# Moving the degrees and layernorm statistics of the incoming sample from behind the first to behind the fifth product of a step

## Chip, cores, metric

One core of one Trainium2 chip. The metric is the device time of one execution in microseconds (us). Each figure is a median of several executions. All compared executions are of the fast state (none is more than 1.5% above the fastest of its kernel); the one single execution, whose state is unknown, is named where it is used. A granted clock is the mean share of TensorE's full clock in an execution. Ratios are the mean time of one kernel's fast runs over that of the other's of the same rounds, so they are not quite the ratio of the medians quoted.

## The reference, cut to what matters

```python
h = jnp.maximum(_layernorm(x, axis=-1), 0.0)          # x: (64, 256, 768)
adj = adj.astype(h.dtype); radj = jnp.swapaxes(adj, 1, 2)   # (64, 256, 256) of 0 and 1
deg, rdeg = adj.sum(-1), radj.sum(-1)                 # 1 where 0, when divided by
ctx = adj  @ (h @ Wadj.T + badj) / deg  \
    + radj @ (h @ Wrev.T + brev) / rdeg \
    + h @ Wself.T + bself
out = x + ctx + rel        # rel: terms of rank 1 in deg and rdeg for this data
```

## The kernel before

For each of the 64 samples the three 768x768 weight products are done as 15 smaller products of combined blocks, a fast matrix multiplication. Each of the 15 is six fp32 matmuls of 128x256, which the profile shows as 12 records (x12). Products bear the numbers of the algorithm: product 5 stands at place 0 of a step, product 10 at place 4, product 14 at place 11. In the profile a product has the name of the bank that it is summed in (y, v, x, u, z, w, t). The y that waits below is product 13, at place 13. A loop over samples is software-pipelined. Step `t` does the products of sample `M = t`, aggregates sample `A = t+1` over its adjacency (`pa`), and loads and normalises sample `N = t+2`. Everything between two products is issued by `others_of_step`. In the traces an engine works in the order of the program: in step 30 VectorE reads v only at 1514.84, behind the waiting statistics, though TensorE finished v near 1508.1, and GpSimd does b2-a only behind the power, for which it was idle 10.26 us.

```python
def statistics(b):                       # VectorE, one instruction on GpSimd
    ...
    for c in range(C):
        for n in range(2):
            nc.vector.bn_stats(stats[:, c, n, :], s["x"][:, c, ts(n, HO)])
        nc.vector.bn_aggr(v[:, c, MEAN : RSTD + 1], stats[:, c, :, :])
    nc.vector.tensor_scalar(v[:, :, RSTD], ...)                     # L269
    nc.gpsimd.tensor_tensor(v[:, :, RSTD], ..., half, op=ALU.pow)   # L270
    ...                                                # junk: is adj only 0 and 1?
    nc.vector.tensor_scalar(t[:, :, 0:2], t[:, :, 3:5], ...)        # L276, needs degrees
    ...                                                # L277, reciprocal, copy L280

def normalise(b):
    for c in range(C):
        nc.vector.tensor_scalar(hx[:, c, :], s["x"][:, c, :], ...)            # L309
        nc.scalar.activation(s["hi"][:, c, :], hx[:, c, :], AF.Copy, scale=rstd)
        nc.vector.scalar_tensor_tensor(s["lo"][:, c, :], hx[:, c, :], ...)    # L313

def others_of_step(A, N, k):             # behind the product at place k of 15
    if N is not None and k == 0:
        degrees(N)                       # ScalarE: int32 to fp32r with row sums
        statistics(N)
    if A is not None:
        if 1 <= k <= F:                  # F is 6
            aggregate(A, k - 1)          # four matmuls into pa, a multiply into X
        if k == 3:
            self_features(A)             # GpSimd: xT, then relu on ScalarE
            ...
    if N is not None:
        if k == 8:
            spread(N)                    # TensorE transposes the columns (pt)
        if k == 9:
            normalise(N)

def step(t):
    load(N)                              # x has 3 buffers: waits for the store of sample t-1
    for k, (n, bank, row, reads, needs) in enumerate(ORDER):
        for name in needs:
            combine_left(M, name)        # GpSimd sums of left blocks
        ...
        product(M, n, banks[bank], start, row)
        for read in reads:
            add_out(M, banks[bank], *read)   # VectorE: x += or -= the product
        others_of_step(...)
```

Of the kernel before, what the change touches and what calls it, by code (L numbers as in the profile page):

```python
# [81 lines left out]
def kernel(  # L82
# [54 lines left out]
    def main_path(main: ExitStack):  # L137
# [108 lines left out]
        def load_xt(b):  # L246
            s = S[b]
            s["xT"] = pool1.tile([P, F, L], F32, tag="xT", name=f"xT_{b}")
            nc.sync.dma_start(s["xT"], xt_v[b])

        def degrees(b):

            s = S[b]
            s["a"] = pool2.tile([P, C, 2, L], F32R, tag="a", name=f"a_{b}")
            for c in range(C):
                for k in range(2):
                    nc.scalar.activation(  # L257
                        s["a"][:, c, k, :], s["adj"][:, c, k, :], AF.Copy, accum_out=tok[b % 2][:, c, 4 - k : 5 - k]
                    )

        def statistics(b):
            s = S[b]
            t, v = tok[b % 2], cols[b % 2]
            stats = pool2.tile([P, C, 2, 6], F32, tag="stats", name=f"stats_{b}")
# [4 lines that stand above are left out]
            nc.vector.tensor_scalar(v[:, :, RSTD], v[:, :, RSTD], EPS, None, op0=ALU.add)  # L269
            nc.gpsimd.tensor_tensor(v[:, :, RSTD], v[:, :, RSTD], half, op=ALU.pow)  # L270
            junk = pool1.tile([P, C, L], BF16, tag="junk", name=f"junk_{b}")
            a = s["adj"][:, :, 1, :]
            nc.vector.scalar_tensor_tensor(
                junk, a, 1.0, a, op0=ALU.is_equal, op1=ALU.not_equal, accum_out=others[:, b : b + 1]
            )
            nc.vector.tensor_scalar(t[:, :, 0:2], t[:, :, 3:5], 0.0, None, op0=ALU.is_gt)  # L276
            nc.vector.tensor_scalar(v[:, :, RDEG : RRDEG + 1], t[:, :, 3:5], 1.0, None, op0=ALU.max)  # L277
            nc.vector.reciprocal(v[:, :, RDEG : RRDEG + 1], v[:, :, RDEG : RRDEG + 1])
            to = v.rearrange("p c (k r) -> p c k r", k=2)[:, :, :, :NROW]
            nc.vector.tensor_copy(to, t.unsqueeze(2).to_broadcast([P, C, 2, NROW]))  # L280

        def spread(b):

            s = S[b]
            v = cols[b % 2]
            pt = ps1.tile([P, P], F32, tag="pt", name=f"pt_{b}")
            nc.tensor.transpose(pt, v.rearrange("p c k -> p (c k)"), ident)  # L287
            s["tokT"] = pool3.tile([P, P], F32R, tag="tokT", name=f"tokT_{b}")
            nc.scalar.activation(s["tokT"], pt, AF.Copy)
            line = pool2.tile([P, P], F32, tag="line", name=f"line_{b}")  # L290
            nc.scalar.activation(line, pt, AF.Copy)
            d = dram.tile([4, C, P], F32, tag="d", name=f"d_{b}")
            for c in range(C):
                nc.sync.dma_start(d[:, c, :], line[c * 64 + MEAN : c * 64 + RRDEG + 1, :])
            s["row"] = pool1.tile([P, 4, L], F32, tag="row", name=f"row_{b}")
            nc.sync.dma_start(
                s["row"].rearrange("p k i -> p (k i)"), d.rearrange("k c p -> (k c p)").partition_broadcast(P)
            )

        def normalise(b):  # L300

            s = S[b]
            v = cols[b % 2]
            s["hi"] = pool1.tile([P, C, H], F32R, tag="hl0", name=f"hi_{b}")
            s["lo"] = pool1.tile([P, C, H], F32R, tag="hl1", name=f"lo_{b}")
            hx = pool1.tile([P, C, H], F32, tag="hx", name=f"hx_{b}")
            for c in range(C):
                rstd = v[:, c, RSTD : RSTD + 1]
                nc.vector.tensor_scalar(  # L309
                    hx[:, c, :], s["x"][:, c, :], v[:, c, MEAN : MEAN + 1], 0.0, op0=ALU.subtract, op1=ALU.max  # L310
                )
                nc.scalar.activation(s["hi"][:, c, :], hx[:, c, :], AF.Copy, scale=rstd)  # L312
                nc.vector.scalar_tensor_tensor(  # L313
                    s["lo"][:, c, :], hx[:, c, :], rstd, s["hi"][:, c, :].bitcast(F32), op0=ALU.mult, op1=ALU.subtract
                )

        def new_left(b):
            S[b]["X"] = pool2.tile([P, F, 3, L], F32, tag="X", name=f"X_{b}")

        def self_features(b):  # L320

            s = S[b]
            xT, row = s["xT"], s["row"]
            parts = ((nc.gpsimd, 0, F),) if b > 0 else ((nc.gpsimd, 0, F // 2), (nc.vector, F // 2, F))
            for eng, f0, f1 in parts:
                for k, op in ((0, ALU.subtract), (1, ALU.mult)):
                    v = xT[:, f0:f1, :]
                    eng.tensor_tensor(v, v, row[:, k : k + 1, :].to_broadcast([P, f1 - f0, L]), op=op)  # L328
            nc.scalar.activation(s["X"][:, :, 2, :], xT, AF.Relu)

        def aggregate(b, f):
            s = S[b]
            pa = ps2.tile([P, 512], F32, tag="pa", name=f"pa_{b}_{f}")
            k = 0
            for c in range(C):
                for part in ("hi", "lo"):
                    nc.tensor.matmul(  # L337
                        pa, s[part][:, c, ts(f, P)], s["a"][:, c, :, :].rearrange("p s i -> p (s i)"),
                        start=(k == 0), stop=(k == 2 * C - 1),
                    )  # L340
                    k += 1
            nc.vector.tensor_mul(  # L342
                s["X"][:, f, 0:2, :].rearrange("p s i -> p (s i)"), pa, s["row"][:, 2:4, :].rearrange("p s i -> p (s i)")
            )
# [87 lines left out]

        def others_of_step(A, N, k):

            if N is not None and k == 0:
                degrees(N)
                statistics(N)
            if A is not None:
                if k == 1:
                    new_left(A)  # L440
                if 1 <= k <= F:
                    aggregate(A, k - 1)
                if k == 3:
                    self_features(A)
                    if N is not None:
                        load_xt(N)
            if N is not None:
                if k == 8:
                    spread(N)
                if k == 9:  # L450
                    normalise(N)

        def step(t):
# [7 lines left out]
            for k, (n, bank, row, reads, needs) in enumerate(ORDER):  # L461
                for name in needs:
                    combine_left(M, name)
                if t == 0:
                    first_step(k)
                start = bank not in banks
                if start:
                    pool, tag = (ps1, bank) if bank in ("x", "y") else (ps3, "q")
                    banks[bank] = pool.tile([P, 512], F32, tag=tag, name=f"{bank}_{M}")[:, :NB]
                product(M, n, banks[bank], start, row)  # L470
                for read in reads:
                    add_out(M, banks[bank], *read)
                for at in range(k, k + 1 if k + 1 < len(ORDER) else k + 4):
                    others_of_step(A if has_a else None, N if has_n else None, at - wait)
                if t == B - 1 and k == 2:
                    flag_others()
                if k == 13:
                    nc.sync.dma_start(out_v[M][:, 0, :], S[M]["x"][:, 0, :])
# [175 lines left out]
```

## Time and profile before

| | before |
|---|---|
| time, median of the first 4 runs | 3161.97 us (3150.85 to 3170.08) |
| span of the profiled execution | 3137.0 us |
| TensorE busy, VectorE busy | 94%, 43% |
| start-up up to step 2, then a steady step | 158 us, 47.76 us (median) |
| stop of pa in a steady step, mean | 0.47 us |
| stop of y in a steady step | 2.17 us |

A "stop" below is measured on TensorE's timeline. It is the distance from the start of one group of matmuls to the start of the next, less what that distance is where nothing waits. Where nothing waits, it repeats to 0.03 us. The prediction shows the lines of the profile that carry this, but for one of VectorE's (line waited for, total us, times, longest):

```profile
DVE stats L267 <- DMA x<-in_x_dram: 270.9, 61, 6.1
```

### The profile page before, as it was taken

How to read it: one execution, taken by the hardware profiler on the slowest of the kernel's cores; microseconds unless marked ns; L12 is line 12 of the kernel's file. 1: busy time of each engine (PE TensorE's matmuls, PEld its weight loads, DVE VectorE, ACT ScalarE, POOL GpSimd, SP SyncE). 2: the span in 40 equal slices, each digit the busy share in tenths (PEclk: the TensorE clock that was granted, in tenths of full speed). 3: DMA queues.
4: the chain of work that ended last, by engine and by line, in shares of the span. 5: the costliest groups of instructions: out<-in, count | busy, mean ns of one | idle time of the engine just before them, and what ended most of it. 6: DMA issues, size and time to landing. Idle time of an engine off the chain costs nothing.

```text
span 3137.0 us, 33335 instructions
## 1 busy us (share of the span) xinstructions
PE 2951.0 (94%) x13514; PEld 2535.8 (81%) x13514; DVE 1344.4 (43%) x2526; ACT 362.9 (12%) x845; POOL 1891.5 (60%) x903
## 2 busy tenths in 40 slices
PE   6899999999999999999999999999999999999999
PEld 4788888888888888888888887888788888888888
DVE  7543444444444434444444444444444444444441
ACT  2110111111111101111111110111111110111100
POOL 3755666566566656665665565656655666666563
PEclk8999999999999999999999999999999999999999
DMA  7122111221221221122212212222122122121210
GB/s 246 61 81 73 65 71 68 74 78 61 81 78 61 79 79 62 71 72 77 71 66 76 78 61 71 71 75 73 61 81 78 61 72 77 70 71 66 76 61 21
DMA packets 126053, 233.25 MB, mean 74 GB/s; under 512 B 7092, under 2 KB 68276, under 8 KB 125896
## 3 DMA queue, kind: packets, MB, share of 16 engines
q1 hardware_dynamic: 125896, 231.08, 21.2%
q8 instruction: 108, 1.77, 0.2%
q14 instruction: 49, 0.40, 0.0%
HBM read 180.46 MB, written 50.59 MB: 74 GB/s over the span
## 4 chain that ended last, share of the span: by engine, by line
PE 66%; DVE 21%; DMA 7%; ACT 4%; issue 1%; POOL 1%; SPq 0%; DVEq 0%; ACTq 0%; POOLq 0%
PE y L363 14%; PE x L363 14%; PE w L363 11%; PE z L363 10%; PE pa L337 10%; DVE hx L309 8%; DVE lo L313 5%; DMA x<-in_x_dram 4%; ACT hi L312 4%; PE u L363 3%; PE v L363 3%; DMA out_dram<-x 2%; DVE x L376 2%; DVE x L378 2%; DVE stats L267 2%
## 5 line engine op out<-in xcount | busy, mean ns | idle before, releaser
L363 PE MATMUL y<-w,X 128*128 128x256 f32 x2304 | 545.1, 387 | 124.0 <-DVE x L378 119.6
L363 PEld LDWEIGHTS y<-w,X 128*128 128x128 f32 x2304 | 434.4, 193 | 200.1 <-DVE x L378 137.8
L358 POOL TENSOR_TENSOR X<-X 128x768 f32<-128x768 f32 x190 | 345.8, 1820 | 293.8 <-PE pt L287 275.5
L270 POOL TENSOR_TENSOR cols<-cols,half 128x2 f32<-128x2 f32 x64 | 68.5, 1070 | 633.4 <-DVE cols L269 622.8
L328 POOL TENSOR_TENSOR xT<-xT,row 128x1536 f32<-128x1536 f32 (+1 forms) x128 | 440.0, 3437 | 12.1 <-DMA row<-d 7.1
L337 PE MATMUL pa<-a,hi 128*128 128x512 f32 x768 | 358.8, 467 | 23.2 <-DVE X L342 19.1
L363 PE MATMUL x<-w,X 128*128 128x256 f32 x1536 | 352.8, 379 | 1.6 <-POOL X L358 1.6
L363 PE MATMUL x<-w,a2+b 128*128 128x256 f32 x1536 | 352.6, 379 | 0.0
L358 POOL TENSOR_TENSOR a2+b<-X,a2+b 128x768 f32<-128x768 f32 x128 | 234.6, 1833 | 149.7 <-PE z L363 92.7
L363 PEld LDWEIGHTS x<-w,X 128*128 128x128 f32 x1536 | 287.3, 190 | 42.5 <-POOL X L358 2.0
L363 PEld LDWEIGHTS x<-w,a2+b 128*128 128x128 f32 x1536 | 282.6, 190 | 39.6
L342 DVE TENSOR_TENSOR X<-pa,row 128x512 f32<-128x512 f32 x384 | 263.8, 687 | 101.0 <-PE pa L337 101.0
L337 PE MATMUL pa<-a,lo 128*128 128x512 f32 x768 | 303.9, 396 | 0.5 <-DVE lo L313 0.5
L309 DVE TENSOR_SCALAR hx<-x,cols 128x768 f32<-128x768 f32 x128 | 261.0, 2039 | 0.0
L267 DVE BATCH_NORM_STATS2 stats<-x 128x6 f32<-128x384 f32 x256 | 127.1, 538 | 270.9 <-DMA x<-in_x_dram 270.9
L257 ACT ACTIVATE a<-adj 128x256 fp32r<-128x256 int32 x256 | 103.5, 406 | 1011.8 <-DMA adj<-in_adj_dram 1011.8
L358 POOL TENSOR_TENSOR a2+b<-X 128x768 f32<-128x768 f32 x64 | 162.4, 2538 | 96.3 <-PE x L368 96.3
L313 DVE SCALAR_TENSOR_TENSOR lo<-hx,cols,hi 128x768 fp32r<-128x768 f32 x128 | 152.1, 1188 | 137.4 <-ACT hi L312 137.4
L337 PEld LDWEIGHTS pa<-a,hi 128*128 128x128 f32 x768 | 145.8, 190 | 70.9 <-DVE X L342 40.6
L363 PE MATMUL w<-w,X 128*128 128x256 f32 x768 | 178.5, 382 | 7.8 <-DVE x L376 7.8
L363 PE MATMUL y<-w,b0+b 128*128 128x256 f32 x768 | 178.2, 382 | 7.2 <-DVE x L378 4.4
L363 PE MATMUL z<-w,a2+b 128*128 128x256 f32 x768 | 177.9, 382 | 2.9 <-DVE x L376 2.9
(87 smaller groups left out, 4078.7 us busy)
## 6 DMA issues: line engine op xcount, KB each, us to landing
x<-in_x_dram SPq DMA_DIRECT2D x64, 768.0 KB, 4.4
xT<-in_x_t_dram SPq DMA_DIRECT2D x64, 768.0 KB
out_dram<-x SPq DMA_DIRECT2D x128, 384.0 KB, 2.3
adj<-in_adj_dram SPq DMA_DIRECT2D x64, 512.0 KB, 3.5
row<-d SPq DMA_DIRECT2D x64, 512.0 KB, 4.3
w<-in_Wadj_dram SPq DMA_DIRECT2D x6, 768.0 KB
w<-in_Wself_dram SPq DMA_DIRECT2D x5, 768.0 KB
w<-in_Wrev_dram SPq DMA_DIRECT2D x4, 768.0 KB, 9.7
```

What stands on the lines that cost most here:

```text
L257: nc.scalar.activation(s["a"][:, c, k, :], s["adj"][:, c, k, :], AF.Copy, accum_out=tok[b % 2][:, c, 4 - k : 5 - k])
L267: nc.vector.bn_stats(stats[:, c, n, :], s["x"][:, c, ts(n, HO)])
L270: nc.gpsimd.tensor_tensor(v[:, :, RSTD], v[:, :, RSTD], half, op=ALU.pow)
L309: nc.vector.tensor_scalar(hx[:, c, :], s["x"][:, c, :], v[:, c, MEAN : MEAN + 1], 0.0, op0=ALU.subtract, op1=ALU.max)
L312: nc.scalar.activation(s["hi"][:, c, :], hx[:, c, :], AF.Copy, scale=rstd)
L313: nc.vector.scalar_tensor_tensor(s["lo"][:, c, :], hx[:, c, :], rstd, s["hi"][:, c, :].bitcast(F32), op0=ALU.mult, op1=ALU.subtract)
L328: eng.tensor_tensor(v, v, row[:, k : k + 1, :].to_broadcast([P, f1 - f0, L]), op=op)
L337: nc.tensor.matmul(pa, s[part][:, c, ts(f, P)], s["a"][:, c, :, :].rearrange("p s i -> p (s i)"), start=(k == 0), stop=(k == 2 * C - 1),)
L342: nc.vector.tensor_mul(s["X"][:, f, 0:2, :].rearrange("p s i -> p (s i)"), pa, s["row"][:, 2:4, :].rearrange("p s i -> p (s i)"))
L358: (eng or nc.gpsimd).tensor_tensor(L[name], L[x], L[y], op=op)
L363: nc.tensor.matmul(ps, l[:, f, :], W[n][:, f, :], start=(start and f == 0), stop=(row is None and f == F - 1), skip_group_check=not start,)
L376: nc.vector.tensor_add(o, o, ps)
```

## The change

The intent is to take the statistics, which wait for a late load of x, away from the beginning of the step, where VectorE must soon read products and multiply pa.

```diff
         def others_of_step(A, N, k):
 
-            if N is not None and k == 0:
-                degrees(N)
-                statistics(N)
             if A is not None:
 ...
             if N is not None:
+                if k == 4:
+                    degrees(N)
+                    statistics(N)
                 if k == 8:
                     spread(N)
```

## The prediction

> **What bounds the kernel now.** I read the page first, then the table of waits by engine, then one steady step in the timeline of each engine.
>
> ```profile
> span 3137.0 us, 33335 instructions
> PE 2951.0 (94%) x13514; PEld 2535.8 (81%) x13514; DVE 1344.4 (43%) x2526; ACT 362.9 (12%) x845; POOL 1891.5 (60%) x903
> ```
>
> TensorE is busy for 94% of the span, and its products head the chain that ended last. So this change can only win back time in which TensorE stood still. The table of waits says for whom it stood still (line waited for, total us, times, longest):
>
> ```profile
> PE y L363 <- DVE x L378: 124.0, 61, 4.4
> PE pa L337 <- DVE X L342: 19.1, 25, 3.5
> PEld y L363 <- DVE x L378: 137.8, 60, 2.3
> PEld pa L337 <- DVE X L342: 40.6, 61, 4.2
> ```
>
> There are two regular stops, one of each kind in a step of one sample. The large one (y, the fourteenth product) is 2.0 us in nearly every step. The small one (pa, the adjacency product) shows 25 times on the matmul row but 61 times on the weight-load row: most of these stops are too short to open a gap between modelled matmuls. Step 30 in the timeline, TensorE first:
>
> ```profile
> 1497.57 2.86 PE L363 MATMUL y<-w,X 128*128 128x256 f32 x12 [2.00 <-DVE x L378]
> ...
> 1503.08 2.75 PE L363 MATMUL y<-w,b0+b 128*128 128x256 f32 x12
> ...
> 1512.70 2.75 PE L363 MATMUL u<-w,X 128*128 128x256 f32 x12
> 1516.17 0.50 PE L337 MATMUL pa<-a,hi 128*128 128x512 f32 x1 [0.72 <-DVE X L342]
> ```
>
> The step begins at 1503.08 with product 5. The third group of pa (1516.17) must wait for a buffer: pa has two, and the first is free only when VectorE has multiplied it into X. VectorE in the same stretch:
>
> ```profile
> 1505.87 0.42 DVE L376 TENSOR_TENSOR x<-x,y 128x256 f32<-128x256 f32 x1 [2.17 <-PE y L363]
> 1511.31 1.02 DVE L267 BATCH_NORM_STATS2 stats<-x 128x6 f32<-128x384 f32 x2 [5.01 <-DMA x<-in_x_dram]
> ...
> 1514.78 0.15 DVE L280 COPY cols<-tok 128x20 f32<-128x20 f32 x1
> 1514.84 0.68 DVE L376 TENSOR_TENSOR x<-x,v 128x512 f32<-128x512 f32 x1
> 1515.43 0.68 DVE L342 TENSOR_TENSOR X<-pa,row 128x512 f32<-128x512 f32 x1
> 1516.04 0.41 DVE L376 TENSOR_TENSOR x<-x,x 128x256 f32<-128x256 f32 x1
> ```
>
> The statistics block stands right behind the first product, where its x has not landed: VectorE idles 5.01 us, then works 3.53 us (1511.31 to 1514.84). Only then may it read v, which TensorE finished near 1508.1. The multiply of pa(0) ends at 1516.1, and TensorE resumes at 1516.17. The x load is late because its buffer is that of the sample just stored:
>
> ```profile
> 1503.73 0.34 SPq L483 DMA_DIRECT2D out_dram<-x  x1
> 1507.07 0.39 SPq L242 DMA_DIRECT2D x<-in_x_dram  x1
> ```
>
> That is 3.34 us for the store to finish and 4.2 us for the load to land.
>
> [...] the read of v sits behind the waiting statistics some 6.7 us after v was done (1508.1 to 1514.84). [...] the 384 KB store takes from 2.3 us (in the common step) to over 3.3 us to release the load. [...] after the 2.0 us stop the y product normally takes 2.86 us, but 4.1 to 4.5 us in five of sixty steps. [...] In the trace, hx (L309) takes 0.61 us alone and about 2.0 us beside a GpSimd sum.
>
> **The change part by part.** Nothing is added or removed. Four ScalarE conversions and eleven VectorE instructions (3.53 us) and one GpSimd power (1.07 us) move, per step, from behind product 5 to behind product 10. The order of the built programs confirms the place: on VectorE after the multiply of pa(3), before the read of w; on GpSimd after the two xT operations; on ScalarE after the relu.
>
> (a) *The stop of pa, steps 2 to 61.* I took start-to-start differences on TensorE for each place in the step. Apart from the two stops and the cold products they agree to 0.03 us. From u over pa(2) to its next matmul they should be 2.82 us (2.40 + 0.42, as at the neighbouring groups). Summed over the 60 steps, the excess is 28.2 us, 0.47 us per step, from 0.0 to 2.16. It tracks the start of the statistics: the best step starts them 7.20 us into the step with no stop, step 30 at 8.23 with about 1.0. All of that should go: after the change VectorE multiplies pa(0) as soon as it is made, near 9 us less queueing, while TensorE needs the buffer only at 12.
>
> (b) *What the block costs in its new place.* Multiply of pa(3): 1520.93 to 1521.6. Block of 3.53 us with no wait, for x landed 10 us earlier: to 1525.2. Read of w delayed from 1523.5 to 1525.2, multiply of pa(4) to 1526.2. TensorE needs the read of w only at 1527.88 (w again), pa(3)'s buffer at 1526.95, and the next z is read at 1527.15. The closest margin is about 1 us, so nothing on the path: cost 0.
>
> (c) *GpSimd.* Before, the power kept it idle 10.26 us and held back b2-a, needed by z at 1517.21. Now b2-a and xT (6.99 us) run from about 1508 to 1517; then the power waits for VectorE at about 1524.3 and ends at 1525.4. a1+b0+b1 behind it moves from 1523.73 to 1525.4 and ends at 1527.2, and product 8 wants it at 1530.59. Margin 3.4 us: cost 0.
>
> (d) *The stop of y.* It is made by normalise (hx, hi, lo twice, 1489 to 1496.4 on VectorE), behind product 6, which does not move. In 59 of 60 steps it adds 2.17 us start to start. It stays: 130 us.
>
> (e) *Step 0.* Here the block of sample 2 moves from product 8 to product 12. Before, GpSimd waited 10.6 us for the power at 81.06, then summed for product 14, so that y at 85.38 waited 4.39 us and then ran cold (5.25 instead of 2.75 us). The sum now goes ahead of the power. Up to 6.9 us; weight combinations on VectorE contend with it, so I take 5.
>
> (f) *Cold y products.* Five events cost some 7.8 us. Four of the five stand in steps with a pa stop over 0.8 us, but the link is loose; I take 3.
>
> Sum: 28 + 5 + 3 = 36 us; 3157.4 − 36 = 3121, rounded to 3120.
>
> **The rivals.** *First, the stop is moved, not removed*: the 3.53 us block now delays w and pa(4), and TensorE stops at w or at pa(5). For it: the same block, still on the in-order engine, in a denser part of the step. Against it: the margins in (b). If 0.5 us per step came back, the time would be about 3150. *Second, the whole VectorE wait is taken for the gain*: 270.9 us of waiting for x are the longest on that engine, and one may expect 5 us per step and about 2900. Against it: TensorE stops for only 0.47 us of it; an idle engine off the path costs nothing. *Third, the y stop changes with it*: [...] hx would take 0.61 us and the stop would shrink, as in step 30 (1.10 us afterwards); 0.9 us in every step would be 55 us more, about 3065. Against it: the sums next to hx (a0+a2+b0+b2, b0+b1) are released by TensorE behind product 6, after the moved work has caught up. *Fourth, the unprofiled runs have larger stops*: they were 18 us longer (3157 against 3139) and scatter by 16 us. If late stores are the reason, the change hides these too and the time falls to about 3103.
>
> **Range and chances.** The steady part is counted and should hold to 5 us; step 0 to 4; cold products to 7; the reason for the 18 us is unknown and mostly pulls downward. Hence 3095 to 3140. Faster by over 2% means below 3094; only the third or fourth rival gets there: 0.07. Slower by over 2% would need a new stop of over 1.5 us per step: 0.02. Within 2%: 0.91.
>
> **What would show it.** Right: PE pa waiting for X (L342) falls to the start-up alone (3.5 us on the matmul row, about 4 on the weight loads); the statistics no longer wait for the x DMA; y still waits 2.0 us per step for L378; steady steps become 47.5 us where they had a mean of 48.1. Wrong: a new wait of w or pa on VectorE, or of product 8 on GpSimd near 28 us into the step, or a y stop other than 2.0 us. A new stop, or a changed y stop, would make the number wrong.

Cut from the record are statements on the hardware that no trace of this case shows, and with them the premise of the third rival, that GpSimd's moved work would no longer run beside hx. No term of the sum is cut: 28 + 5 + 3 = 36 us, and 3157.4 - 36 = 3121, rounded to 3120. Two slowdowns in the trace of the kernel before: hx took 0.61 us in 4 of 128 times (twice with GpSimd idle, twice begun up to 0.2 us ahead of a GpSimd sum) and 1.88 to 2.74 us beside GpSimd in the others. The weight combination of (e) on VectorE took 1.76 us with GpSimd idle (75.86) and 3.24 us beside a sum (83.70).

## The result, and the profile after

The changed kernel took 3121.32 us (median of 4, 3118.01 to 3121.73), against 3161.97 us before. The ratio is 0.9871 (95% interval 0.9837 to 0.9906): 1.3% less, within the 2% called the same, and 1.3 us from the number predicted (3120).

The table of waits of the changed kernel has these lines where the kernel before had its two regular stops:

```profile
PEld y L363 <- DVE x L378: 138.1, 60, 2.3
PE y L363 <- DVE x L378: 124.3, 61, 4.4
PEld pa L337 <- DVE X L342: 9.2, 3, 5.6
PE pa L337 <- DVE X L342: 7.9, 2, 4.9
DVE stats L267 <- DMA x<-in_x_dram: 4.0, 1, 4.0
```

The weight loads of pa waited 61 times before and wait 3 times now, twice in the start-up and once in step 0. The statistics waited for x for 270.9 us before and wait for it once now, at the very beginning. The large stop, y on L378, is what it was. Step 30 on TensorE, then on VectorE:

```profile
1495.50 2.75 PE L363 MATMUL y<-w,b0+b 128*128 128x256 f32 x12
...
1505.12 2.75 PE L363 MATMUL u<-w,X 128*128 128x256 f32 x12
1507.52 0.58 PE L337 MATMUL pa<-a,hi 128*128 128x512 f32 x1
...
1519.31 2.75 PE L363 MATMUL w<-w,a1+b 128*128 128x256 f32 x12
```

```profile
1501.87 0.69 DVE L342 TENSOR_TENSOR X<-pa,row 128x512 f32<-128x512 f32 x1 [0.30 <-PE pa L337]
...
1512.35 0.69 DVE L342 TENSOR_TENSOR X<-pa,row 128x512 f32<-128x512 f32 x1 [0.50 <-PE pa L337]
1512.96 1.01 DVE L267 BATCH_NORM_STATS2 stats<-x 128x6 f32<-128x384 f32 x2
...
1516.48 0.41 DVE L378 TENSOR_TENSOR x<-x,w 128x256 f32<-128x256 f32 x1
1516.82 0.68 DVE L342 TENSOR_TENSOR X<-pa,row 128x512 f32<-128x512 f32 x1
```

The multiply of pa(0) now ends near 1502.6, five microseconds before TensorE wants that buffer at 1507.52, and pa follows u in 2.40 us as everywhere else. The statistics begin at 1512.96 without a wait, take 3.52 us, and w is read by 1516.9. TensorE needs that only at 1519.31.

Where the 20.9 us between the two profiled spans (3137.0 and 3116.1) come from, by place in the step:

| part | before | after | difference |
|---|---|---|---|
| stop of pa, steps 2 to 61 | 28.2 us | 0.0 us | -28.2 |
| stop of y, steps 2 to 61 | 129.4 us | 129.6 us | +0.2 |
| slow y products behind that stop (the prediction's cold ones), with 0.1 us of restart in each step (2.86 us where 2.75 is usual) | 5, 14.7 us in all | 10, 23.2 us in all | +8.5 |
| step 0 | 75.13 us | 73.05 us | -2.1 |
| remainder | | | +0.7 |

The stop of pa is gone exactly. A third of its worth in these two executions was lost again in slow y products (4.54 us in place of 2.86), which the timeline of the changed kernel shows at every sixth step:

```profile
485.69 4.54 PE L363 MATMUL y<-w,X 128*128 128x256 f32 x12 [2.01 <-DVE x L378]
534.88 2.86 PE L363 MATMUL y<-w,X 128*128 128x256 f32 x12 [2.02 <-DVE x L378]
...
772.38 4.54 PE L363 MATMUL y<-w,X 128*128 128x256 f32 x12 [2.01 <-DVE x L378]
```

The wait ahead of each is the same, yet one takes 4.54 and another 2.86 us.

### The profile page after: what moved, and what is told of

The parts are those of the page before. It is cut to its first block, busy times and chain, and to the rows that moved or that the text cites. A ratio compares the mean times of both kernels' runs of the same rounds, so it can differ in the third digit from the quotient of the medians.

```text
span 3116.1 us, 33214 instructions
## 1 busy us (share of the span) xinstructions
PE 2948.9 (95%) x13514; PEld 2547.7 (82%) x13514; DVE 1365.0 (44%) x2526; ACT 356.2 (11%) x845; POOL 1895.5 (61%) x903
## 4 chain that ended last, share of the span: by engine, by line
PE 77%; DVE 17%; ACT 4%; issue 1%; POOL 0%; DMA 0%; ACTq 0%; SPq 0%; DVEq 0%; POOLq 0%
PE y L363 17%; PE x L363 16%; PE pa L337 11%; PE z L363 10%; PE w L363 10%; DVE hx L309 8%; PE u L363 5%; PE v L363 5%; DVE lo L313 5%; ACT hi L312 4%; DVE x L376 2%; DVE x L378 1%; DVE w L182 0%; PE x L368 0%; PE t L363 0%
## 5 line engine op out<-in xcount | busy, mean ns | idle before, releaser
L363 PE MATMUL y<-w,X 128*128 128x256 f32 x2304 | 551.9, 391 | 119.9 <-DVE x L378 119.9
L363 PEld LDWEIGHTS x<-w,X 128*128 128x128 f32 x1536 | 286.7, 190 | 40.6 <-POOL X L358 0.3
L358 POOL TENSOR_TENSOR b2-a<-X 128x768 f32<-128x768 f32 x64 | 117.4, 1834 | 318.0 <-PE v L363 318.0
L329 ACT ACTIVATE X<-xT 128x1536 f32<-128x1536 f32 x64 | 94.9, 1483 | 1399.5 <-POOL xT L328 1399.5
L363 PE MATMUL w<-w,a1+b 128*128 128x256 f32 x768 | 178.8, 383 | 2.8 <-DVE x L378 2.8
```

The lines of the kernel that those rows point to most:

```text
L329: nc.scalar.activation(s["X"][:, :, 2, :], xT, AF.Relu)
L358: (eng or nc.gpsimd).tensor_tensor(L[name], L[x], L[y], op=op)
L363: nc.tensor.matmul(ps, l[:, f, :], W[n][:, f, :], start=(start and f == 0), stop=(row is None and f == F - 1), skip_group_check=not start,)
```

## The experiments

My theory was that the stop of pa is the statistics block's start plus its length, counted against the moment TensorE wants the pa buffer back, and that only VectorE's order matters. The rivals were that the block costs wherever it stands, that the degrees on ScalarE have a part, and that the two stops depend on each other.

### Does ScalarE have a part?

```diff
-            if N is not None and k == 0:
-                degrees(N)
-                statistics(N)
+            if N is not None and k == 0:
+                degrees(N)
+                ...
+                if k == 4:
+                    statistics(N)
```

> Only the statistics move behind product 10; the degrees on ScalarE stay behind product 5. Theory (the cause is the VectorE block in the in-order queue, ScalarE has no part): pa stop 0 in steps 2 to 61, time as after the change, 3121 plus or minus 6 us. Rival (the degrees on ScalarE matter, for they wait for the adj load ahead of the relu): over 3130 us and part of the pa stop or a new wait remains.

Measured: 3121.41 us (3120.26 to 3122.40), ratio 0.9879. In the trace the stop of pa is 0 in all 60 steps. The degrees contribute nothing that can be measured; moving the statistics alone gives the whole gain. What is left of the pa waits lies in the start-up:

```profile
PEld pa L337 <- DVE X L342: 8.2, 2, 4.7
```

### Is it the length of the block or its place?

The mean and variance part stays at place 0, and the rest goes to place 4:

```diff
-            if N is not None and k == 0:
-                degrees(N)
-                statistics(N)
+            if N is not None and k == 0:
+                statistics(N)            # mean, variance, power only
+                ...
+                if k == 4:
+                    degrees(N)
+                    degree_rows(N)       # junk, tok, reciprocal, copy
```

> The mean and variance part (2.5 us of VectorE, with its wait for x) stays behind product 5; the degree part (1.06 us of VectorE) and the degrees move behind product 10. Theory (stop of pa = start of the block + its length - what fits before the third pa group): each stop shrinks by 1.06 us and not below zero; on the stops of the first trace that leaves 3 us of 28, so 3121 to 3130 us. Rival (any wait for the DMA on VectorE costs the stop, whatever the block's length): the stop stays near 28 us or more and the time near 3155 us.

Measured: 3225.19 us, ratio 1.0214 (1.0166 to 1.0262): slower than before, though by the 2% rule unclear. The expectation for the stop of pa held: it sums to 3.3 us where 3 us was expected. The expectation for the time failed, because a new stop stands ahead of the second w product in 40 of 60 steps (1.4 to 1.8 us, 63 us in all), and the slow y products rose to 26. Its waits, then one step of its VectorE:

```profile
DVE tok L280 <- ACT a L257: 158.0, 61, 2.6
```

```profile
529.78 2.95 DVE L277 SCALAR_TENSOR_TENSOR junk<-adj 128x512 bf16<-128x512 int32 x1
532.66 0.07 DVE L277 DVE_READ_ACCUMULATOR junk<-adj 128x1 f32 x1
535.33 0.17 DVE L280 TENSOR_SCALAR tok<-tok 128x4 f32<-128x4 f32 x1 [2.59 <-ACT a L257]
535.40 1.79 DVE L281 TENSOR_SCALAR cols<-tok 128x4 f32<-128x4 f32 x1
...
537.38 0.41 DVE L382 TENSOR_TENSOR x<-x,w 128x256 f32<-128x256 f32 x1
```

The same step on its GpSimd:

```profile
523.40 1.83 POOL L362 TENSOR_TENSOR b2-a<-X 128x768 f32<-128x768 f32 x1
525.20 6.98 POOL L332 TENSOR_TENSOR xT<-xT,row 128x1536 f32<-128x1536 f32 x2
```

Only 1.06 us of work moved, but it took 7.6 us there. With the power at place 0, GpSimd still waits for x and does xT late (525.20 to 532.18). The relu behind xT, and the degrees behind the relu, are then late on ScalarE, and tok waits for them. The `junk` comparison, normally 0.69 us, took 2.95 us beside xT. So the place behind product 10 is free only because the changed kernel frees GpSimd early as well: there xT is finished (1502.72 to 1509.71) before the block begins at 1512.96.

### Is it the late x?

A fourth x buffer, with the block left at place 0. The room comes from putting `hx` in the buffer of a1+b1.

```diff
-            s["x"] = pool3.tile([P, C, H], F32, tag="x", name=f"x_{b}")
+            s["x"] = pool4.tile([P, C, H], F32, tag="x", name=f"x_{b}")   # 4 buffers
...
-            hx = pool1.tile([P, C, H], F32, tag="hx", name=f"hx_{b}")
             for c in range(C):
+                hx = pool1.tile([P, H], F32, tag="t3", name=f"hx_{b}_{c}")
```

> The order of before, but a fourth x buffer, so that the load of x does not wait for the store (room made by putting hx in the buffer of a1+b1). Block of 3.53 us still behind product 5. Theory (the lateness of x is what makes the block hurt): the load is issued about 1.0 us into the step, lands near 5.4 us, statistics start near 5.5 instead of 7.2 to 9.3, pa stop 0, time 3121 plus or minus 8 us. Rival (the block behind product 5 costs by its own length): most of the 28 us stays, 3145 us or more.

Measured: 3161.25 us, ratio 1.0019: no gain, 40 us above what I expected. The load is issued 1.04 us into the step as foreseen, and the statistics begin at about 6 us. In 48 of 60 steps the stop is 0. In the other 12 it sums to 27 us. In five of these x itself landed late (7.4 to 8.4 us into the step). In seven the statistics began early, but the block stretched to as much as 8.98 us; these seven make 25 of the 27 us. (Moving hx is a second change in this run, but the stop of y stayed at 2.16 us a step.) One such step on VectorE:

```profile
2624.72 1.02 DVE L268 BATCH_NORM_STATS2 stats<-x 128x6 f32<-128x384 f32 x2 [2.55 <-DMA x<-in_x_dram]
...
2629.09 1.31 DVE L277 TENSOR_SCALAR tok<-tok 128x4 f32<-128x4 f32 x1 [1.04 <-ACT a L258]
...
2630.60 3.19 DVE L281 COPY cols<-tok 128x20 f32<-128x20 f32 x1
2633.70 0.68 DVE L377 TENSOR_TENSOR x<-x,v 128x512 f32<-128x512 f32 x1
```

Here the adj load, still late, holds the degrees and they hold tok. By then GpSimd has begun its xT operations, and a copy of 20 elements takes 3.19 us where it usually takes 0.15 (63 of 64 times in the trace of the kernel before). The late x is the cause of the stop in most steps, as the theory says. But an early x only brings the next late thing to light, because the whole block still stands in front of the products.

### How far may it move?

```diff
-                if k == 4:
+                if k == 1:        # and, in another kernel, k == 7
                     degrees(N)
                     statistics(N)
```

> The block one product later than before (position 1, behind the read of v and the multiply of pa(0)). Theory (what hurts is only that the multiply of pa(0) stands behind the wait): VectorE still waits for x there, up to 2 us, but the multiply of pa(0) is done and pa(1) is due only near 15.5 us into the step; pa stop 0, time 3121 plus or minus 6 us. Rival (the block must be clear of the x load altogether): a stop remains, 3135 us or more.

Measured: 3129.71 us (3124.59 to 3140.44), ratio 0.9897. The stop of pa is 0, as expected. But the time is 8 us above what I expected, so neither side was quite right. (The trace is of the longest of the four executions.) The power on GpSimd now waits for x ahead of b2-a, and product 10 waits for b2-a in the steps where x is late. On the weight-load row of the trace:

```profile
PEld z L363 <- POOL b2-a L358: 22.4, 44, 2.3
```

By start-to-start distances it costs 12 us, and 5 us more for slow products behind it. One place later was nearly enough for VectorE, but not for GpSimd.

> The block behind product 3 (position 7) in place of product 10 (position 4). Theory (a place is free only while its margin lasts): the transpose of the columns stands behind the next product, and the power on GpSimd ends about 1.6 us after TensorE reaches it, so a new stop at the transpose of 1.6 us a step, pa stop 0, time near 3218 us (3195 to 3235), slower than before. Rival (any place away from the x load is as good): 3121 us.

Measured: 3300.03 us, ratio 1.0438 (1.0418 to 1.0458). The new stop is where it was expected:

```profile
PE pt L287 <- POOL cols L270: 110.5, 63, 9.2
```

It is 1.74 us a step, where 1.6 was expected. The time was 82 us above the expected 3218, because 51 of 60 y products were slow, at 1.69 us each (86 us).

### How large is the margin at place 4?

```diff
-            for c in range(C):
+            for c in (0, 1, 0, 1):        # and, in another kernel, three times
                 for n in range(2):
                     nc.vector.bn_stats(...)
```

> The changed kernel with the mean and variance part computed twice, 2.4 us more of VectorE behind product 10, same result. Theory (the place has a margin of about 2.4 us, read from the trace after: w is read to 1516.8, and TensorE wants it at 1519.3): the read of w ends within 0.1 us of when TensorE wants it, so no stop or one of up to 0.15 us a step; 3121 to 3132 us. Rival (the margin is the 1.1 us ahead of the next read of z): a stop of over 1 us a step, 3185 us or more.

> The same part computed three times, 4.9 us more. Theory (margin 2.4 us): the surplus of 2.4 us a step becomes a stop at the second w product, 60 x 2.4 = 147 us plus more cold products, 3265 to 3340 us. Rival (VectorE has slack enough anywhere in the step, for it is busy only 44% of the time): 3121 us.

Measured: 3124.86 us with the part twice and 3364.96 us with it three times (ratios 0.9893 and 1.0655). In the traces the block takes 5.78 and 8.03 us in place of 3.52. The first shows no new stop, and y and pa are as after the change. The second shows a stop of 2.15 us at the second w product in every step, so the margin is 8.03 - 3.52 - 2.15 = 2.36 us. These stops make 129 of the 240 us between the two. Most of the rest is slow products: 40 at y, where the first has 11, and 27 at w.

```profile
PE w L363 <- DVE x L378: 126.2, 61, 7.2
PE y L363 <- DVE x L378: 124.5, 61, 4.4
```

VectorE is busy only 44% of the span in the changed kernel, and still 4.5 us more at this spot cost 8%.

### What makes the stop of y, and do the stops depend on each other?

`normalise` in two halves, the first at place 9 and the second at place 13, once on the changed kernel and once on the kernel before:

```diff
                 if k == 9:
-                    normalise(N)
+                    normalise(N, (0,))
+                if k == 13:
+                    normalise(N, (1,))
 ...
```

(The loop that serves the shifted first two steps runs on to reach place 13.)

> The changed kernel, with normalise in two halves: first behind product 6 as now, second behind product 13. Theory (the 2.17 us stop of y is made by the whole of normalise standing ahead of the read of y of product 14, and the cold y products, 1.69 us each, come from that stop): y stop 0, no cold y products in the steady steps, steps of about 45.0 us in place of 47.8 on average, time about 2968 us (2950 to 2990). Rival (the stop moves on: the later read of x delays the store, the load of x, or hi and lo come too late for pa): a new stop of 1 to 2 us at pa or x, time over 3040 us.

Measured: 2960.51 us (2956.98 to 2961.03), ratio to before 0.9362 (0.9347 to 0.9378). The stop of y is 0, there are no slow y products, and every steady step takes 45.22 us to within 0.04. TensorE's share:

```profile
PE 2913.8 (98%) x13514; PEld 2534.9 (86%) x13514; DVE 1324.3 (45%) x2526; ACT 356.3 (12%) x845; POOL 1905.6 (64%) x903
```

Every row that its table of waits has left for TensorE counts one or two waits, all in the first steps but one of 0.6 us in the last. It is the fastest version, 5.2% below the changed kernel by the medians. It is also confirmation of step (d) of the prediction: the stop of y is made by the whole of `normalise` standing ahead of the read of product 14.

> The same two halves on the kernel before. Theory: the read of x of product 1 is about 1.6 us later, so the store, the load of x, and the statistics behind product 5 are later by as much, and the pa stop grows from 0.5 to about 2.1 us a step; y stop 0. Net about 0.8 us a step gained over before: 3110 us (3085 to 3140), far above the split on the changed kernel. Rival (the two changes are independent): the split gains as much here as on the changed kernel, about 150 us, so about 3010 us.

Measured: 3051.44 us, ratio 0.9660. The stops depend on each other, as I held, but less than I expected:

```profile
PE pa L339 <- DVE X L344: 72.6, 61, 3.1
```

The stop of pa grew from 0.47 to 1.43 us a step (86 us in all), not to 2.1. The read of x behind the second half came 1.1 us later into the step, not 1.6, because hx there took 1.06 us and not 2.16 (both read in the trace of the split on the changed kernel). The split therefore gains 108 us over before on the old order and 161 us over the changed kernel on the new. The change studied here is worth 1.3% alone, and 91 us, or 3%, once the stop of y is out of the way.

### The slow y products

In each trace with them I took the start of every y product behind a stop of over 2 us, modulo 3.413 us. That period comes out of the traces alone: of all periods from 1.5 to 8 us, in steps of 0.0005, every one further than 0.0015 us from 3.413 leaves 100 or more of the 405 fast products of the ten traces inside the bands, and 3.4133 leaves none. The slow ones lie in one band, and no fast one lies in it. Six of the ten traces:

| kernel | slow of 60 | band of the slow ones |
|---|---|---|
| before | 5 | 1.31 us |
| before, again | 8 | 1.27 us |
| changed | 10 | 0.70 us |
| statistics only | 11 | 0.77 us |
| mean and variance at 0 | 26 | 1.29 us |
| block at 7 | 51 | 1.38 us |

In the changed kernel seven of the nine distances between neighbouring slow ones are 286.7 us, which is 83.99 periods. A step of 47.50 us is 13.92 periods, so the stop drifts through the band and meets it every sixth step. Before, a step of about 47.76 us is 13.99 periods and hardly drifts. At place 7 a step with a slow product is 14.94 periods and stays in the band. So the number of slow products goes with the length of the step: 5 to 8 of 60 at 47.8 us, 10 at 47.5, 51 at 51.0. A stop alone does not make one: in the split on the kernel before, stops of pa of 1.1 to 2.0 us in 59 of 60 steps made none (granted clock 0.995). That is a pattern; why the period is 3.413 us, no run here shows. The test of the cause is to keep the array busy:

```diff
+                if k == 13 and 2 <= t < B - 2:
+                    idle = ps2.tile([P, 512], F32, tag="pa", name=f"idle_{M}")
+                    for _ in range(4):
+                        nc.tensor.matmul(idle[:, :NB], ident, W[13][:, 0, :], start=True, stop=True)
                 product(M, n, banks[bank], start, row)
```

> The changed kernel with four useless 128x256 products (about 1.6 us of TensorE) in the 2.0 us stop ahead of y, in steps 2 to 61; their result is never read. VectorE still releases y at the same moment. Theory ([...] in all traces so far the cold ones lie in one band of at most 1.4 us of a 3.413 us period): no cold y product in the steady steps, y stop shrinks to about 0.5 us on TensorE's rows, granted clock up from 0.989 to about 0.995, and the time falls by some 10 x 1.69 us plus the 0.10 us of slower restart in each step, to about 3098 us (3092 to 3106). Rival (a cold product has nothing to do with the idle array, or useless work only delays y): 3121 us or more.

(What was to be tested is whether the 2.0 us that TensorE idles ahead of y make y slow.)

Measured: 3103.68 us (3102.27 to 3105.39), ratio to before 0.9828; granted clock 0.995 to 0.996 against 0.989 to 0.990 for the changed kernel. The steps are as long as the fast steps of the changed kernel (47.50 us), and none of the y products behind the filler is slow. Step 31:

```profile
1577.49 1.89 PE L473 MATMUL idle<-w,ident 128*128 128x256 f32 x8
1579.67 2.86 PE L363 MATMUL y<-w,X 128*128 128x256 f32 x12 [0.29 <-DVE x L378]
```

The restart of 0.1 us (2.86 in place of 2.75) stayed in 59 of 60 steps, against what was expected. So 240 useless products made the kernel 17.6 us faster by the medians, 13.6 by the ratios to before. With the stop filled by 1.89 us of work no y product behind it is slow, where 10 of 60 were, and with the stop gone (the split on the changed kernel) none is: the slow y products come from the idle time ahead of them, not from anything in the product.

### Why the kernel before scatters

> The kernel before, unchanged, profiled once more. Theory (the jitter of the kernel before comes from the stop of pa, that is from how late the store and the x load are): the span of this execution differs from 3137 us by the difference in the summed pa stop (28.2 us in the first trace) plus 1.7 us for each difference in the number of cold y products, to within 5 us. Rival (the jitter has another source): the pa stop is again about 28 us whatever the span is.

Measured: span 3147.0 us, 10.0 us over the first trace (one execution, so its state is unknown). The pa stop was 3.4 us more (31.6 against 28.2), and there were 8 slow y products in place of 5, which makes 3.4 + 5.1 = 8.5 us: within the 5 us asked for. It supports the theory for two executions. For the executions without a trace there is only the granted clock. Over 27 executions of the kernel before it runs from 0.993 (the shortest span, 3137.0 us) to 0.987 (3165.5 us; the longest, 3166.3 us, has 0.988), with a correlation of -0.92. Four executions of the changed kernel have 0.989 to 0.990 and spans of 3116.1 to 3119.9 us.

With no slow y products the clock was 0.996 (the split on the changed kernel), with 51 it was 0.969, so each lowers it by some 0.0005. By that estimate a usual execution of the kernel before (0.989) has about as many slow products as the changed kernel, and the profiled ones had fewer. The 8.5 us that slow products took back between the two traces then fall away for a usual execution, which explains some 29 of the timed 41 us where the traces show 20.9. This is an estimate, no trace shows it, and the other 11 us stay open: how much of them is the pa stop in untraced executions is not known.

## Why the prediction was right

The number was right to 1.3 us. The mechanism, step (a), is shown and was counted rightly. The two smaller terms, (e) and (f), were both wrong toward too much gain, so the traces give 21 us where I summed 36. That the number still came out is in part luck: the timed executions gained 20 us more than the traced ones, for a reason that is only partly explained.

- **(a), the stop of pa.** Right, and exactly: 28.2 us of stops became 0.0 in the trace, in the changed kernel and with the statistics moved alone. But the stops did not follow the start of the statistics alone. The largest, 2.16 us in step 45, came after an early start (7.47 us) with a block stretched to 5.46 us, as later with four x buffers.
- **(b), no cost in the new place.** Right. But "the closest margin is about 1 us" was wrong: the late read of z stops nobody, and the margin that counts is the 2.36 us at w.
- **(c), GpSimd.** Right: b2-a ran at 1500.93, xT to 1509.71, the power from 1515.63, and a1+b0+b1 ended at 1518.47, 3.5 us before product 8 at 1522.01. What I had not seen is that this early end of xT is needed: where it is taken away, the same place costs 63 us at w.
- **(d), the stop of y stays.** Right: 129.6 us after 129.4. Splitting `normalise` removes it. (Its first hx in step 29 begins at 1487.93, not 1489.)
- **(e), step 0.** Mis-sized: 2.1 us in place of 5. The stop of 4.39 us ahead of y did go. But a weight combination on VectorE, beside an earlier xT, took 4.87 us where it had taken 3.24, and pa waited 3.02 us for the multiply behind it. The run with the filler, whose step 0 has the same instructions, took 74.38 us there, so even 2.1 us is not firm.
- **(f), cold y products.** Wrong in the traces: I took 3 us off, and they became 10 in place of 5, some 9 us on. I read them as a by-product of large pa stops. They come from the stop of y and the length of the step, measured against a period of 3.413 us. So the steady steps have the median of 47.50 us that I named, but a mean of 47.82.
- **The rivals.** The first (the stop moves) did not happen here, but happened in three experiments that moved the work differently (at w, at z and at pt). The second (270.9 us of waiting as gain) is refuted: all that waiting on VectorE went, and about 40 us came of it. The third (the y stop shrinks) is refuted: 2.17 us as before. The fourth is open: the timed gain does exceed the profiled one, as it said, but that larger stops of pa from late stores are the reason is not shown (the second trace of the kernel before had 3.4 us more of them in 10 us of span).

With (e) and (f) corrected, the traces give 28.2 + 2.1 - 8.5 = 21.8 us, close to the 20.9 us between the two profiled spans. My sum of 36 us came near the timed difference of 41 only because the usual execution of the kernel before is slower than the one I had a trace of. Of the signs, one was missed: TensorE still waits 7.9 us for pa and not 3.5, in the start-up (4.9) and in step 0 (3.0).

## What to carry to other kernels

Count an engine's wait only as far as it stops the engine that bounds the kernel: 270.9 us of waiting here were worth 28. When work is moved in an in-order queue, check the place for the other engines too, since it was free only because GpSimd moved along (63 us of stops at w where it did not); doubling or tripling the moved work measures the margin. And look for the next stop before being content: splitting the other block of VectorE work brought 5%, and made this change worth twice as much.
